# A graph layer's node products: from a scheduler's order to the order as written

## The chip, the cores and the metric

The kernel runs on one core of a Trainium2 chip. The metric is the device time of one launch in microseconds; the median of three timed runs of the kernel before is 6621.72 us (6620.99 to 6621.94). The profile was taken in an execution of its own, which with the profiler running spans 7287.9 us. Comparisons are made in timed runs; the profile serves to see where time lies.

Names of the engines: PE is TensorE (matmuls), PEld its loads of weights, DVE is VectorE, ACT is ScalarE, POOL is GpSimd, SP is SyncE, which only starts transfers here.

## The reference

10,000 nodes with 512 features, 160,000 edges sorted by destination, four edge types. Cut to what matters:

```python
# layer 0
h = relu(layernorm(x))
h_all = einsum('nd,rdf->nrf', h, rel_W) + rel_b        # four products for each node
agg = segment_sum(h_all[src, edge_type], dst) / max(deg, 1)
u = layernorm(h + h @ self_W + self_b + agg) * ln1_w + ln1_b
out = layernorm(u + gelu(u @ W1 + b1) @ W2 + b2) * ln2_w + ln2_b
x = x + out
# layer 1: two rounds of h <- relu(h @ W_self + mean of h[src] over a node's edges @ W_neigh + b)
x = x + layer1(relu(layernorm(x)))
```

All is in fp32. The nodes are handled in 79 blocks of 128 (the last has 16).

## The kernel before

It has four stages: (1) the node products, with the work on the edges put between them: for each block of nodes five products of 128x512 by 512x512, one with `self_W` and four with `rel_W`, whose results go to memory, and beside it the lists of rows that each block will gather; (2) gathering and summing for layer 0 and its feed-forward part; (3) and (4) the two rounds of layer 1, which gather again. Stages 2 to 4 are bound to the order in which they are written. Stage 1 isn't: a scheduler orders its instructions and puts each engine's queue together by its own model of their times.

The edge work is a Python generator: each `next(step)` emits the instructions up to the next `yield`. First `runs`, which finds where each node's edges begin, then `lists`. The parts of stage 1 that matter:

```python
    def runs(ep, ep2, pse, found):
        # ... loads of dst, dst shifted by one, src, etype
        yield
        # ... d_f, m, ends, bad: each wants the loads; then keys
        for i in range(ROUNDS):                     # ROUNDS = 12: the largest eight keys of a row, 12 times
            nc.vector.max(out=top[:, w], in_=key)
            # ... match_replace takes them out of key
            if i % 2:
                yield
        # ...
        pn = pse.tile([P, 512], F32, name="pe")
        for i in range(ROUNDS):                     # counting
            w = slice(8 * i, 8 * i + 8)
            inb = ep2.tile([P, 8, NB], F32, name="inb")
            nc.vector.tensor_tensor(inb, ..., op=OP.is_equal)
            inl = ep2.tile([P, 8, P], F32, name="inl")
            nc.vector.tensor_tensor(inl, ..., op=OP.is_equal)
            nc.vector.tensor_tensor(inl, inl, ..., op=OP.mult)
            for j in range(8):
                nc.tensor.matmul(pn[:NB, :P], inb[:, j, :], inl[:, j, :], start=(i + j == 0),
                                 stop=(i == ROUNDS - 1 and j == 7))
            if i % 2:
                yield
        # ... scans over the counts, bounds of each block, two levels, the test `fits`

    def look_up(b0, nb, win):                       # two blocks of the list
        # ... marks and own rows, on VectorE
        for c in range(nb):
            nt = OT if b0 + c < full else OT_LAST
            of = between(found["from"], found["upto"], b0 + c, nt * P, "of")     # two masks
            pm = pse.tile([P, OT, WT], F32, name="pe")
            for t in range(nt):
                nc.tensor.matmul(pm[:, t, :], of[:, t * P:(t + 1) * P],
                                 halves[:, c, 2 * t0:2 * t0 + WT], start=True, stop=True)
            got, rows, none = picked(pm[:, :nt], slot[:, :nt], 0, 2)             # eleven small operations
            nc.vector.tensor_tensor(loc[:, b0 + c, :nt], got[:, :, 1], none, op=OP.add)
            nc.vector.tensor_copy(orow[:, b0 + c, :nt], rows)
        # ...
        for c in range(nb):
            # ... kept <- a part of the window; masks `beyond` for two levels (4 and 16 blocks)
            #     at the last block of a level: share(lv, b)

    def share(lv, last):
        # ...
        for j in range(n):
            nc.tensor.matmul(pm[:, 0, :], beyond[lv][:, j, :], kept[0][:, (b1 + j) % SPAN, :],
                             start=(j == 0), stop=(j == n - 1))
        got, rows, none = picked(pm[:, :1], slot[:, :1], 64, 4 + 2 * lv)
        # ... stores to srow and loc
```

And the loop that drives it:

```python
        def products(g):
            b0, nb, r = g
            xg = loaded.pop()
            sc = norm_scales(ap_, [xg[:r, c, :] for c in range(nb)], r, "a")
            hg = xp.tile([P, 4, D], F32, name="hg")
            for c in range(nb):
                h = hg[:r, c, :]
                nc.scalar.activation(h, xg[:r, c, :], AF.Relu, bias=sc[c][1], scale=sc[c][0])
                hT = ap_.tile([P, KC, P], F32, name="hT")
                transposed(psT, hT[:, :, :r], h, r)
                nc.vector.tensor_tensor(h, h, bself[:r], op=OP.add)
                nc.vector.tensor_tensor(xg[:r, c, :], xg[:r, c, :], ln2b[:r], op=OP.add)
                ha = ap_.tile([P, R, D], F32, name="ha")
                for j, w in enumerate([wself] + wrel):
                    pm = psM.tile([P, D], F32, name="pm")
                    for k in range(KC):
                        nc.tensor.matmul(pm[:r], hT[:, k, :r], w[:, k, :], start=(k == 0),
                                         stop=(k == KC - 1))
                    if j:
                        nc.vector.tensor_tensor(ha[:r, j - 1, :], pm[:r],
                                                brel[:r, (j - 1) * D:j * D], op=OP.add)
                    else:
                        nc.vector.tensor_tensor(h, pm[:r], h, op=OP.add)
                n0 = (b0 + c) * P
                nc.scalar.dma_start(hall_d[n0:n0 + r, :], ha[:r].rearrange("p r d -> p (r d)"))
                gate[:] = [ha[:, 0, :1]] if r == P else []
                if b0 + c >= 2:
                    next(step, None)
            nc.sync.dma_start(rows_of(xs_d, g), hg[:r, :nb])
            nc.sync.dma_start(rows_of(xr_d, g), xg[:r, :nb])

        for g, later in zip(groups, groups[1:] + [None]):
            products(g)
            if later:
                load(later)
        gate.clear()
        for _ in step:
            pass
```

`norm_scales` is two statistics instructions per block on VectorE, a square root on ScalarE and two small instructions on VectorE for a group of four blocks; `transposed` is four transposes on TensorE and one copy on ScalarE. The accumulators `pm` have four buffers, `hT` and `ha` two each, the edge work's `pe` two.

After the stage every engine loads `fits`, the test whether the lists have room, and branches to stages 2 to 4:

```python
    go = nc.values_load(fits[0:1, 0:1], min_val=0, max_val=1, ...)
    with tc.If(go > 0) as cmp:
        with ExitStack() as ctxa:
            with tc.manual_schedule():
                aligned(ctxa)
```

Of the kernel before, what the change touches and what calls it, by code (L numbers as in the profile page):

```python
# [8 lines left out]
F32 = mybir.dt.float32  # L9
# [12 lines left out]
def kernel(  # L22
# [52 lines left out]


    T = 11 * E // (16 * N)
    OT = 5
    OT_LAST = 3
# [3 lines left out]

    ROUNDS = 12
    PAD = P

    W = 36
    TAGS = 4 + 3 * NL
    FAR = 2 * SPAN * P
    WT = 2 * W + TAGS  # L90
    assert N % P and R * N <= 1 << 16 and 2 * T + WT <= 2 * P and OT * WT <= 512
    assert (4 + 3 * NL) * NB <= 1024 and 3 * NL * NB <= 512
    assert 4 * OT * P <= R * N and OT_LAST < OT and full % 2 == 0

    def own(b):

        return T if b < full else 0

# [24 lines left out]


    row = const.tile([P, full, T], I32, name="row")
    orow = const.tile([P, NB, OT], I32, name="orow")
    srow = [const.tile([P, -(-full // n)], I32, name=f"srow{i}") for i, n in enumerate(SPANS)]
    loc = const.tile([P, NB, OT + NL], F32, name="loc")
# [41 lines left out]
    def runs(ep, ep2, pse, found):  # L170
# [32 lines left out]
        yield  # L203
# [30 lines left out]
        for i in range(ROUNDS):  # L234
            w = slice(8 * i, 8 * i + 8)
            nc.vector.max(out=top[:, w], in_=key)
            if i + 1 < ROUNDS:
                rest = ep2.tile([P, EC], F32, name="m")
                nc.vector.match_replace(out=rest, in_to_replace=top[:, w], in_values=key,
                                        imm_value=0.0)  # L240
                key = rest
            if i % 2:
                yield
# [29 lines left out]
        for i in range(ROUNDS):  # L273
# [14 lines left out]
            if i % 2:  # L288
                yield
# [18 lines left out]
        nc.vector.tensor_tensor(deg, first[:, 1:], first[:, :P], op=OP.subtract)  # L308

# [25 lines left out]
        bounds = ep.tile([NB, 3 * NL, P], F32, name="bounds")  # L335
        nc.vector.tensor_copy(first_over, over)
        done = 0
        for lv, n in enumerate(SPANS):
# [22 lines left out]
            for i, v in enumerate((ov, upto)):  # L361
                w = bounds[:, 3 * lv + i, :]
                nc.vector.tensor_scalar(w, bounds[:, 3 * lv - 3 + i, :] if lv else v,
                                        float(-P if lv else -OT * P), 0.0, op0=OP.add, op1=OP.max)
                nc.vector.tensor_scalar(w, w, skip, None, op0=OP.add)
            nc.vector.tensor_scalar(bounds[:, 3 * lv + 2, :], ov, shift, 64.0, op0=OP.add,
                                    op1=OP.add)
            nc.vector.tensor_scalar(bounds[:, 3 * lv + 2, :], bounds[:, 3 * lv + 2, :], 0.0, None,
                                    op0=OP.max)
            yield  # L370
        for names, vs in ((("first", "deg", "from", "upto"), (first[:, :P], deg, ov, upto)),
                          ([f"{k}{lv}" for lv in range(NL) for k in ("sfrom", "supto", "sbase")],
                           [bounds[:, i, :] for i in range(3 * NL)])):
# [6 lines left out]
        nc.vector.memset(bad[:, 3:5], 0.0)  # L380
# [3 lines left out]
        nc.vector.tensor_scalar(bad[:NB, 3:4], upto_b, float(-P), over, op0=OP.is_lt, op1=OP.add)  # L384
        nc.vector.tensor_reduce(room, deg, op=OP.max, axis=mybir.AxisListType.X)
        nc.vector.tensor_tensor(room, room, lanes_b, op=OP.subtract)
        nc.vector.tensor_scalar(bad[:NB, 4:5], room, float(W), None, op0=OP.is_gt)
        pf = pse.tile([P, 512], F32, name="pe")
        nc.tensor.matmul(pf[:1, :5], ones[:, :1], bad, start=True, stop=True)
        count = ep.tile([1, 1], F32, name="count")  # L390
        nc.vector.tensor_reduce(count, pf[:1, :5], op=OP.add, axis=mybir.AxisListType.X)
        nc.vector.tensor_scalar(fits, count, 0.0, None, op0=OP.is_equal)
# [4 lines left out]
    def lists(ep, ep2, pse, found):  # L397

        tags = ep.tile([P, NB, TAGS], F32, name="tags")
        tag_i = ep.tile([P, NB, TAGS - 2], I32, name="tag_i")  # L400
        nc.vector.memset(tags[:, :, 0:1], 1.0)
        nc.gpsimd.iota(tags[:, :, 1], pattern=[[0, NB]], base=0, channel_multiplier=1,
                       allow_small_or_imprecise_dtypes=True)
        for i, n in enumerate(SPANS):
            of = tag_i[:, :, 2 + 2 * NL + i]
            nc.gpsimd.iota(of, pattern=[[1, NB]], base=0, channel_multiplier=0)
            nc.vector.tensor_scalar(of, of, n - 1, None, op0=OP.bitwise_and)
        for i, name in enumerate(["from"] + [f"sbase{lv}" for lv in range(NL)]):
            hi, lo = tag_i[:, :, 2 * i], tag_i[:, :, 2 * i + 1]
            nc.vector.tensor_copy(lo, found[name])  # L410
            nc.vector.tensor_scalar(hi, lo, 4, None, op0=OP.logical_shift_right)
            nc.vector.tensor_scalar(lo, lo, 15, None, op0=OP.bitwise_and)
        nc.vector.tensor_copy(tags[:, :, 2:], tag_i)
        nc.vector.memset(orow[:, full:, :], 0)
        nc.vector.tensor_scalar(rdeg, found["deg"], 1.0, None, op0=OP.max)
        nc.vector.reciprocal(rdeg, rdeg)
        iota_s = ep.tile([P, OT * P], F32, name="iota_s")
        nc.gpsimd.iota(iota_s, pattern=[[1, OT * P]], base=0, channel_multiplier=0,
                       allow_small_or_imprecise_dtypes=True)
        of_span = ep.tile([P, SPAN], F32, name="of_span")  # L420
        nc.gpsimd.iota(of_span, pattern=[[P, SPAN]], base=0, channel_multiplier=0,
                       allow_small_or_imprecise_dtypes=True)
        slot = ep.tile([P, OT], F32, name="slot")
        nc.gpsimd.iota(slot, pattern=[[P, OT]], base=0, channel_multiplier=1,
# [73 lines left out]
        def look_up(b0, nb, win):  # L498
# [24 lines left out]
            if not t0:  # L523
                return
# [819 lines left out]
```

## Time and profile before

| | |
|---|---|
| timed, median | 6621.72 us |
| profiled span | 7287.9 us |
| first stage, to its last VectorE instruction | about 1578 us |
| busy over the whole span | PE 77%, DVE 50%, ACT 14%, POOL 52% |
| eviction of a product (`ha<-pm,brel`, 128x512) | 688 ns, x312 |
| bias addition (`hg<-hg,bself`) and residual addition (`xg<-xg,ln2b`) on DVE | 684 and 683 ns, x78 each |
| lookup mask (`of<-iota_s,f_upto,after`, 128x640) | 878 ns, x78 |

A group in the profile reads: line, engine, operation, output<-inputs, shape, count | busy us in all, mean ns of one | us that the engine stood idle before it <- what it waited for. A wait reads: engine, tile and line that waited <- who released it: total us, times, longest. A timeline row reads: start us, length us, engine, line, operation, count. The product matmuls are in fp32 and each appears as two records, so a product of four matmuls is eight records.

### The profile page before, as it was taken

To read this page: it belongs to the slowest core of one execution; us is meant where nothing else is said; L and a number is where in the kernel's file an instruction comes from. 1 tells how busy PE (TensorE), PEld (TensorE's weight loads), DVE (VectorE), ACT (ScalarE), POOL (GpSimd) and SP (SyncE) were. 2 spreads that over 40 slices of the span, in tenths; PEclk is the share of its full clock that TensorE was granted. 3 is DMA by queue.
4 is the path that set the end of the run, shared out by engine and by line. 5 is a ranking of instruction groups with operands and counts; after the bars stand their busy time and mean duration, and the time that the engine had idled before them with its cause. 6 is when DMAs were issued, how large, how long until landed. Compare 5 with 4: busy or idle time off the path is not lost.

```text
span 7287.9 us, 49954 instructions
## 1 busy us (share of the span) xinstructions
PE 5630.5 (77%) x14251; PEld 2543.5 (35%) x14251; DVE 3658.1 (50%) x7302; ACT 1016.8 (14%) x1667; POOL 3806.5 (52%) x3927
## 2 busy tenths in 40 slices
PE   8999999976899888897676666666666666666666
PEld 3444444433334333343333233333232233332232
DVE  5457777334666666665344344333333444444444
ACT  1000000002233223232211011001010000000000
POOL 0000010026666666666266666666656666666665
PEclk9999999987999999998888888888887888887888
DMA  4222222246677777776366666666666777777775
GB/s 156 101 99 99 104 94 93 93 142 191 214 222 225 227 218 225 225 228 207 125 199 207 207 207 208 207 207 204 207 205 206 218 220 218 218 217 216 221 220 171
DMA packets 456993, 1361.47 MB, mean 187 GB/s; under 512 B 71746, under 2 KB 71746, under 8 KB 446578
## 3 DMA queue, kind: packets, MB, share of 16 engines
q0 software_dynamic: 308768, 1008.91, 46.8%
q1 hardware_dynamic: 136146, 266.29, 10.3%
q10 hardware_dynamic: 11792, 82.97, 2.8%
q8 instruction: 114, 1.87, 0.1%
q14 instruction: 173, 1.42, 0.1%
HBM read 1150.89 MB, written 207.01 MB: 186 GB/s over the span
## 4 chain that ended last, share of the span: by engine, by line
PE 34%; issue 21%; another core or an unknown queue 19%; ACT 3%; DVE 3%; POOL 2%; DMA 2%; ACTq 0%; POOLq 0%; DVEq 0%; SPq 0%
PE pa L687 9%; PE ph L783 6%; PE pm L620 5%; PE po L794 5%; PE po L991 3%; PE po L1025 3%; DVE pa L699 2%; POOL rows L660 2%; PE pT L167 1%; ACT hTb L168 1%; DMA rows<-h_d,row 1%; ACT mTb L168 1%; ACT mb L1021 0%; PE pT L771 0%
## 5 line engine op out<-in xcount | busy, mean ns | idle before, releaser
L699 DVE TENSOR_TENSOR pa<-pa,rows 128x512 f32<-128x512 f32 x2574 | 1798.6, 699 | 906.1 <-issue 571.5
L660 POOL DMA_INDIRECT rows<-h_d,row x1716 | 1669.4, 973 | 906.0 <-issue 423.0
L1025 PE MATMUL po<-wss,hTb 128*128 128x512 f32 (+1 forms) x1264 | 710.5, 715 | 652.1 <-ACT hTb L168 536.3
L687 PE MATMUL pa<-rows,hot 128*128 128x512 f32 (+1 forms) x2358 | 1096.2, 611 | 55.5 <-issue 31.9
L660 POOL DMA_INDIRECT rows<-hall_d,row x858 | 855.9, 998 | 492.6 <-issue 196.3
L620 PE MATMUL pm<-wrel,hT 128*128 128x512 f32 (+1 forms) x2528 | 1101.0, 593 | 14.4 <-DVE ha L623 14.4
L991 PE MATMUL po<-wns,mTb 128*128 128x512 f32 (+1 forms) x1264 | 662.0, 673 | 439.0 <-ACT mTb L168 306.3
L660 POOL DMA_INDIRECT rows<-h_d,orow x786 | 754.6, 960 | 400.8 <-issue 218.9
L620 PEld LDWEIGHTS pm<-wrel,hT 128*128 128x128 f32 (+1 forms) x2528 | 478.0, 189 | 622.1 <-issue 595.9
L687 PEld LDWEIGHTS pa<-rows,hot 128*128 128x128 f32 (+1 forms) x2358 | 458.9, 195 | 665.2 <-issue 631.6
L783 PE MATMUL ph<-x1T,w1s 128*128 128x512 f32 (+2 forms) x1344 | 587.0, 590 | 117.9 <-ACT hid L785 88.4
L1025 PEld LDWEIGHTS po<-wss,hTb 128*128 128x128 f32 (+1 forms) x1264 | 277.8, 231 | 1024.0 <-ACT hTb L168 589.5
L660 POOL DMA_INDIRECT rows<-hall_d,orow x393 | 373.3, 950 | 450.3 <-SPq L1340 326.5
L794 PE MATMUL po<-w2s,hid 128*128 128x512 f32 (+1 forms) x1264 | 560.9, 595 | 30.5 <-issue 23.2
L991 PEld LDWEIGHTS po<-wns,mTb 128*128 128x128 f32 (+1 forms) x1264 | 266.8, 216 | 816.2 <-issue 483.0
L687 PE MATMUL pa<-tail,hot 128*128 128x512 f32 x936 | 469.0, 617 | 78.0 <-issue 72.7
L997 DVE TENSOR_TENSOR po<-po,bss 128x512 f32<-128x512 f32 (+1 forms) x79 | 55.0, 696 | 805.5 <-remote 705.9
L493 POOL DMA_INDIRECT win<-rec_d,at x79 | 74.9, 948 | 719.7 <-issue 631.4
L623 DVE TENSOR_TENSOR ha<-pm,brel 128x512 f32<-128x512 f32 (+1 forms) x316 | 217.1, 687 | 424.1 <-PE pm L620 424.0
L783 PEld LDWEIGHTS ph<-x1T,w1s 128*128 128x128 f32 x1344 | 259.8, 201 | 414.1 <-issue 311.4
L1001 DVE TENSOR_TENSOR ob<-po,bss 128x512 f32<-128x512 f32 (+1 forms) x79 | 54.5, 689 | 663.4 <-remote 293.6
L794 PEld LDWEIGHTS po<-w2s,hid 128*128 128x128 f32 (+1 forms) x1264 | 236.2, 190 | 313.4 <-issue 301.8
(238 smaller groups left out, 4165.3 us busy)
## 6 DMA issues: line engine op xcount, KB each, us to landing
hall_d<-ha ACTq DMA_DIRECT2D x78, 1024.0 KB
hb<-h_d SPq DMA_DIRECT2D x38, 1024.0 KB
rows<-h_d,row POOLq DMA_INDIRECT x1716
xs<-xs_d SPq DMA_DIRECT2D x39, 512.0 KB
xr<-xr_d SPq DMA_DIRECT2D x39, 512.0 KB
xn_d<-xr SPq DMA_DIRECT2D x39, 512.0 KB
h_d<-h SPq DMA_DIRECT2D x39, 512.0 KB
xg<-in_x_dram SPq DMA_DIRECT2D x19, 1024.0 KB
```

What stands on the lines that cost most here:

```text
L167: nc.tensor.transpose(p[:, k, :r], rows[:, k * P:(k + 1) * P], ident[:r, :r])
L168: nc.scalar.copy(dest, p[:, :, :r])
L493: nc.gpsimd.indirect_dma_start(out=win[:, c, :], out_offset=None, in_=rec_d, in_offset=bass.IndirectOffsetOnAxis(ap=at[:, c:c + 1], axis=0))
L620: nc.tensor.matmul(pm[:r], hT[:, k, :r], w[:, k, :], start=(k == 0), stop=(k == KC - 1))
L623: nc.vector.tensor_tensor(ha[:r, j - 1, :], pm[:r], brel[:r, (j - 1) * D:j * D], op=OP.add)
L660: nc.gpsimd.indirect_dma_start(out=t[:n], out_offset=None, in_=table, in_offset=bass.IndirectOffsetOnAxis(ap=idx, axis=0))
L687: nc.tensor.matmul(pa[:r], hot[:, t, :r], others[t], start=(t == order[0]), stop=(t == order[-1]))
L699: nc.vector.tensor_tensor(pa[:r], pa[:r], t[:r], op=OP.add)
L783: nc.tensor.matmul(ph[:, :n], w1s[:, k, f * P:(f + 1) * P], self.xT[:, k, :n], start=(k == 0), stop=(k == KC - 1))
L794: nc.tensor.matmul(po[:r], self.hid[:, f, c * r:(c + 1) * r], w2s[:, f, :], start=(f == 0), stop=(f == FC - 1))
L991: nc.tensor.matmul(po[:r], mT[:, k, :r], wns[:, k, :], start=False, stop=(k == KC - 1))
L1025: nc.tensor.matmul(po[:r], hT[:, k, :r], wss[:, k, :], start=(k == 0), stop=False)
```

## The change

It makes the first stage follow the order in which it is written (`manual_schedule`), and rewrites the loop for it: a block's products come one after another; behind product 0 the next block's norm is prepared, behind product 1 the norm is applied, behind product 3 the next block is transposed; behind products 0, 2 and 4 a piece of edge work is put. The additions of `bself` and of `ln2b` go to GpSimd. The stores of `ha` go from ScalarE's queue to SyncE's. It is meant to keep TensorE going from product to product.

```diff
     with ExitStack() as s:
+        s.enter_context(tc.manual_schedule())
 ... (load, then three new helpers)
+        def stats(g, c):
+
+            if c == 0:
+                scales[g] = norm_scales(ap_, [xgs[g][:g[2], k, :] for k in range(g[1])], g[2], "a")
+
+        def normed(g, c):
+            r = g[2]
+            if c == 0:
+                hgs[g] = xp.tile([P, 4, D], F32, name="hg")
+            nc.scalar.activation(hgs[g][:r, c, :], xgs[g][:r, c, :], AF.Relu, bias=scales[g][c][1],
+                                 scale=scales[g][c][0])
+            nc.gpsimd.tensor_tensor(xgs[g][:r, c, :], xgs[g][:r, c, :], ln2b[:r], op=OP.add)
+
+        def turned(g, c):
+            r = g[2]
+            hTs[g, c] = ap_.tile([P, KC, P], F32, name="hT")
+            transposed(psT, hTs[g, c][:, :, :r], hgs[g][:r, c, :], r)
 ... (products(g) and its loop go)

+        for do in (stats, normed, turned):
+            do(*seq[0])
+        for i, (g, c) in enumerate(seq):
+            n0 = (b0 + c) * P
+            if c == 0 and i + nb < len(seq):
+                load(seq[i + nb][0])
+
+            ahead = {0: stats, 1: normed, 3: turned} if i + 1 < len(seq) else {}
+            h, hT = hgs[g][:r, c, :], hTs.pop((g, c))
+            ha = ap_.tile([P, R, D], F32, name="ha")
+            for j, w in enumerate([wself] + wrel):
+                pm = psM.tile([P, D], F32, name="pm")
+                for k in range(KC):
+                    nc.tensor.matmul(pm[:r], hT[:, k, :r], w[:, k, :], start=(k == 0),
+                                     stop=(k == KC - 1))
+                if j in ahead:
+                    ahead[j](*seq[i + 1])
+                if j:
+                    nc.vector.tensor_tensor(ha[:r, j - 1, :], pm[:r],
+                                            brel[:r, (j - 1) * D:j * D], op=OP.add)
+                else:
+                    nc.vector.tensor_tensor(h, pm[:r], h, op=OP.add)
+                    nc.gpsimd.tensor_tensor(h, h, bself[:r], op=OP.add)
+                if i >= 3 and j % 2 == 0:
                     next(step, None)
+            nc.sync.dma_start(hall_d[n0:n0 + r, :], ha[:r].rearrange("p r d -> p (r d)"))
+            if i == 2:
+                gate[:] = [ha[:, 0, :1]]
+            if c == nb - 1:
+                nc.sync.dma_start(rows_of(xs_d, g), hgs[g][:r, :nb])
+                nc.sync.dma_start(rows_of(xr_d, g), xgs[g][:r, :nb])
```

The edge work is cut into smaller pieces. In `runs`, ten empty pieces stand behind the loads, and both loops over the rounds yield each time:

```diff
-        yield
+        for _ in range(10):
+            yield
 ...
-            if i % 2:
-                yield
+            yield
```

`look_up` becomes two steps for each block, `start` (all its masks) and `finish` (the matmuls and what follows), each a piece of its own:

```diff
+        def finish(self, b, of, window):
+
+            ls = self.ls
+            t0, nt = 2 * ls.own(b), ls.others(b)
+            window = window[:, t0:t0 + ls.WT]
+            pm = self.bank()
+            for t in range(nt):
+                nc.tensor.matmul(pm[:, t, :], of[:, t * P:(t + 1) * P], window, start=True, stop=True)
+            got, rows, none = self.picked(pm[:, :nt], self.slot[:, :nt], 0, 2)
+            nc.vector.tensor_tensor(ls.loc[:, b, :nt], got[:, :, 1], none, op=OP.add)
+            nc.vector.tensor_copy(ls.orow[:, b, :nt], rows)
+            if b == full:
+                return
+            j = b % SPAN
+            if j == 0:
+                self.kept = self.ep.tile([P, SPAN, ls.WT], BF16, name="kept")
+            nc.vector.tensor_copy(self.kept[:, j, :], window)
+            for lv, span in enumerate(SPANS):
+                if b % span == span - 1 or b == full - 1:
+                    self.share(lv, b)
 ...
         def look_up(b0, nb, win):
-            halves = win.rearrange("p b j -> p (b j)").bitcast(BF16).rearrange(
-                "p (b j) -> p b j", b=2)[:, :nb]
 ...
+            halves = halves_of(win, nb)
+            look.mark(b0, nb, halves)
+            if b0 < full:
+                look.mine(b0, nb, halves, found["deg"])
+            of = []
             for c in range(nb):
 ...
+                of.append(look.start(b0 + c))
+                yield
             for c in range(nb):
 ...
+                look.finish(b0 + c, of[c], halves[:, c, :])
+                yield
 ...
         ahead = []
         for b in range(0, NB, 2):
             ahead.append(read(b))
             if len(ahead) > 3:
-                look_up(*ahead.pop(0))
+                yield from look_up(*ahead.pop(0))
             yield
         while ahead:
-            look_up(*ahead.pop(0))
-            yield
```

The test `fits`, computed behind the bounds before, is computed in a last piece behind the lists:

```diff
+    def room(ep, pse):
+
+        pf = pse.tile([P, 512], F32, name="pe")
+        nc.tensor.matmul(pf[:1, :5], ones[:, :1], bad, start=True, stop=True)
+        count = ep.tile([1, 1], F32, name="count")
+        nc.vector.tensor_reduce(count, pf[:1, :5], op=OP.add, axis=mybir.AxisListType.X)
+        nc.vector.tensor_scalar(fits, count, 0.0, None, op0=OP.is_equal)
+        yield
```

The rest of the diff gathers the sizes of a list into a class and passes it along; stages 2 to 4 keep their operations and their order.

## The prediction

> **What bounds the kernel now.** I read the page's slices first, then the windows, the groups by shape, TensorE's waits, and at last the timeline of TensorE and of VectorE. All of the change lies in the first stage, the node products, which end at 1578 us of a profiled span of 7288 us (the timed median is 6621.7 us). The page's first two rows of slices:
>
> ```profile
> PE   8999999976899888897676666666666666666666
> ...
> PEclk9999999987999999998888888888887888887888
> ```
>
> One slice is 182 us, so the stage is the first eight to nine digits: TensorE is at nine tenths at nearly full clock. The windows split the stage (columns: us; busy us and instructions of PE, PEld, DVE, ACT, POOL; clock; DMA share; GB/s):
>
> ```profile
> 300.00:420.00 120.00, 119.35 (x416) 63.24 (x414) 55.79 (x80) 8.72 (x14) 0.00 (x0) 1.00 0.23 88
> 600.00:800.00 200.00, 185.04 (x564) 85.55 (x563) 148.16 (x626) 11.82 (x20) 17.80 (x19) 0.96 0.24 91
> 1400.00:1500.00 100.00, 99.12 (x248) 44.93 (x247) 23.82 (x37) 5.04 (x8) 0.00 (x0) 1.00 0.19 79
> ```
>
> With little VectorE work TensorE idles under 1%; between 600 and 1200 us, where the lists of edges are looked up, it idles 7.5%. TensorE sets this stage, VectorE is at 75% at most. The stage's TensorE waits, from 20 us to 1578 us:
>
> ```profile
> PE pe L518 <- DVE both L466: 53.5, 18, 3.3
> PE pm L620 <- DVE ha L623: 14.4, 1, 14.4
> PE pm L620 <- ACT hT L168: 9.4, 15, 5.2
> PE pe L547 <- DVE both L466: 3.2, 4, 2.5
> ```
>
> That is 80.5 us: all that a perfect order could give back directly. What one stop does is seen in TensorE's timeline:
>
> ```profile
> 817.22 0.52 PE L518 MATMUL pe<-win,of 128*128 128x82 bf16 x5 [2.95 <-DVE both L466]
> 817.54 5.10 PE L620 MATMUL pm<-wself,hT 128*128 128x512 f32 x8
> 822.48 13.90 PE L620 MATMUL pm<-wrel,hT 128*128 128x512 f32 x32
> 859.25 0.36 PE L518 MATMUL pe<-win,of 128*128 128x82 bf16 x5 [2.95 <-DVE both L466]
> 859.45 3.67 PE L620 MATMUL pm<-wself,hT 128*128 128x512 f32 x8
> ```
>
> A product is 8 records, 3.43 us. After a stop of 2.95 us the next takes 5.1 to 5.4 us in 14 of 18 cases and 3.67 us in the others: a stop costs itself and mostly 1.6 us of slower clock.
>
> **What the Trainium skill says.** "TensorE: Matmul & The Clock Gate", Part 1: the array falls to half clock after an idle window of about 3.4 us and needs a busy one to return; a product of twice the time for part of a window is what the lines above show. "PSUM — Partial Sum Buffer", Engine vs sequencer instructions: VectorE, ScalarE and GpSimd queues are strict FIFO and matmuls start in program order; so an edge matmul that waits for VectorE holds all products behind it. The later stages of this kernel, already written out by hand, show VectorE in exactly the written order. "GPSIMD Engine Reference", 3.1 Elementwise: a two-input fp32 addition takes GpSimd 1.96 times VectorE's time; with 0.69 us here an estimate is 1.35 us, and no such addition of GpSimd is in this trace. "SBUF — State Buffer", two separate sides: such an addition excludes a VectorE instruction with two SBUF inputs while it runs; not shown in this trace either.
>
> **What the change removes.** (1) The four waits: 80.5 us. Transposes of the next block come after product 3 and are copied during product 4; the lookup is split so that its masks are made at least one product before the matmul that needs them; ten empty steps cover the load of the edges, for which VectorE stood 22.7 us while TensorE lost 14.4. (2) Slow restarts: 14 x 1.65 = 23 us, and 2.8 us after the long stop (9.83 us for 16 records instead of 7.03): 26 us. (3) Two additions of 0.68 us per block leave VectorE: 79 x 1.37 = 108 us of busy time, worth nothing directly, as VectorE isn't the bound. Sum: 106 us.
>
> **What it adds.** The order as written puts each piece of edge work on VectorE behind the eviction of the product just made, and the piece's matmuls on TensorE before the next product. Where a piece makes a matmul's operand in the same piece, TensorE now stands through a round trip. The rows that price it:
>
> ```profile
> L283 DVE TENSOR_TENSOR inl<-inl,end_f 128x1024 f32<-128x1024 f32 x12 | 14.6, 1217 | 0.1
> L280 DVE TENSOR_TENSOR inl<-lane,to_f 128x1024 f32<-128x1024 f32 x12 | 14.6, 1217 | 0.0
> L276 DVE TENSOR_TENSOR inb<-lane,blk_f 128x632 f32<-128x632 f32 x12 | 9.8, 813 | 4.6 <-PE pe L286 4.6
> ```
>
> (a) The twelve rounds of counting. Eviction starts 0.20 us after the next product could, occupies 0.60; the three instructions start 0.74, 1.25 and 1.22 us apart, as 315.03, 318.02 and 319.27 us of the timeline show; 0.04 to the matmul: 4.05 us of lost products, x 12 = 49 us. Before, the scheduler made the operands one round ahead and TensorE lost nothing (119.35 of 120 us).
>
> (b) The steps from counts to bounds: three VectorE-TensorE round trips, and two for the levels: about 1.6 + 0.7 + 0.9 + 4.3 + 1.5 = 9 us from scans of 0.42 us and small instructions of 0.15 to 0.3 us.
>
> (c) The shared tails. Once in four blocks the piece that finishes a block goes on to a sum over `kept`, whose last part is copied by the last instruction of that piece. Chain behind the eviction (0.80 us): got 0.20, nth twice 0.16, pick 0.34, both 0.53, two reductions 0.33 overlapping to 0.62, five small ones of 0.16 of which three in a chain, two stores and the copy 0.18, with 0.04 between dependent ones: 3.0 us. Less the 0.19 us of the block's own matmuls: 3.7 us lost. 18 of 20 fall inside the stage: 67 us. The second level comes straight behind and finds its operands ready.
>
> (d) Collisions: some of these pieces stand at product 0, where the norm of a group (about 4 us) or GpSimd's addition (1.35 us) is in the way. Three or four shared tails and a third of the rounds: 8 us, a guess.
>
> (e) Slow restarts after 12 + 4 + 18 = 34 stops, at the rate seen now (26 us for 19 stops, 1.4 each): 47 us.
>
> (f) The end. I counted the pieces. The first part has 10 + 3 + 12 + 1 + 12 + 3 = 41, the lists 1 + 40 + 39 x 4 + 2 = 199, the last test 1: 241. Slots: blocks 3 to 78, three each, 228. Thirteen pieces are left when the last product is done: finishing six blocks, beginning five, three shared tails, the test. Six finishes of 3.4 us (the chain and its matmuls), five beginnings of 1.3 to 2.6 us (0.55 + 0.88 us for the large masks, twice 0.29 + 0.34 for the small, 0.4 for marks and rows) make 10.7, three shared tails 2.8, test 1: 41 us. The gathers and the branch wait for that test, which today is known at 457 us, and the first gather comes 3.8 us after the last eviction:
>
> ```profile
> 1577.63 0.68 DVE L623 TENSOR_TENSOR ha<-pm,brel 16x512 f32<-16x512 f32 x1 [2.75 <-PE pm L620]
> 1587.72 0.69 DVE L750 TENSOR_TENSOR lnb<-lnb,h 128x512 f32<-128x512 f32 x1 [9.41 <-DMA ln1wc<-in_L_gnn_ln_w_dram]
> ```
>
> Sum added: 49 + 9 + 67 + 8 + 47 + 41 = 221 us. Net: 221 - 106 = +115 us. The later stages are the same code and only start later: 6622 + 115 = about 6736 us, 1.7% slower.
>
> **The rivals.** *It gains.* If TensorE doesn't really wait in (a) and (c), because queues run ahead or the pieces' operands are ready, only the 106 us remain against a tail: 6622 - 106 + 41 = 6557 us, 1% faster. For it speaks that lookup matmuls were deliberately separated from their masks; against it that counting rounds and shared tails were not. *VectorE falls behind.* If pieces take longer than the gaps between products, four accumulators fill and TensorE stops more: lists need 11 us of VectorE per five pieces, that is 6.6 us per block, with 3.5 us of evictions and 1 us of norm 11 of 18 us; so no lasting backlog, only (d). If it happened, another 40 us: 6780. *The end is hidden.* If the leftovers overlap the last products, or GpSimd's gathers are slow to start anyway, (f) vanishes: 6695. Against: the branch waits for the test, and no part of the gathering stage can begin before it. *Nothing changes*, as the time is set by the gathers: against, because a later start moves everything behind it.
>
> **Range and chances.** (a) and (c) are the firm part, from counted pieces and measured durations; (d), (e) and the overlap inside (f) carry perhaps 20 us each, and the step that TensorE waits at all could fail, but rarely. 8 in 10: 6670 to 6790. The line for 2% is 6754 us, 18 us above my number, so slower by over 2% has 0.36; faster by over 2% would take 132 us, more than all that can be removed: 0.02; within 2%: 0.62.
>
> **What would show it.** In the profile after: the stage ends near 1690 us instead of 1578; TensorE's waits no longer name the lookup's matmul behind the reduction, nor the transposed block, but the counting matmul behind its operands 12 times near 4 us, and the shared sum behind `kept` 18 times near 3.7; the last eviction of a product is followed by some 41 us with TensorE nearly empty and VectorE busy. I am wrong if those stops are absent or short, if the lists are done before the last product, or if the stages behind differ in length by more than some 20 us.

## The result and the profile after

| | before | after |
|---|---|---|
| timed, median | 6621.35 us (6615.35 to 6621.94) | 6777.56 us (6775.24 to 6778.60) |
| last eviction of a product begins | 1577.63 us | 1687.02 us |
| first gather begins | 1582.08 us | 1733.10 us |
| TensorE's stops while it makes products | 80.5 us | 152.2 us |

The change makes the kernel slower: the ratio is 1.0238 (95%: 1.022 to 1.0255), +156 us where +115 was predicted. The first gather, with which the first stage ends, begins 151.0 us later. The stages behind it take 5043.8 us; a second profile of the kernel before has 5039.8 us there. One caution for all that follows: the stages behind the first gather took 5.04 ms on some chips and 5.7 ms on others whichever kernel ran (in the first profile of before 5.7 ms), so variants are compared with before on their own chip in timed runs, and by the start of the first gather in the profiles. The 7287.9 us that stand ahead of the prediction as the profiled span are of this kind and don't come of the profiler: before takes 7285 and 7332 us in timed runs on two of the chips used below, and 6617 to 6628 us on the two others. On the first two the same microseconds make a ratio that is a tenth nearer to 1.

The slices of the page of after (169 us each, the first stage is the first ten and a part of the eleventh):

```profile
PE   8789999998499999999977777777777777777777
...
PEclk9889999999699999999988898888888888898888
```

Two places have changed: the second digit, where the rounds are counted, has fallen to 7 at a lower clock, and the eleventh (1694 to 1863 us) is at 4, with a clock of 6: it holds 39 us without products, in which TensorE waits for the lists, and then the beginning of the gathering. Windows of the two (us; busy us and instructions of PE, PEld, DVE, ACT, POOL; clock; DMA share; GB/s):

```profile
220.00:450.00 230.00, 165.23 (x479) 93.44 (x479) 92.21 (x181) 9.29 (x15) 23.14 (x22) 0.82 0.16 60
...
1687.00:1733.00 46.00, 5.27 (x55) 3.38 (x55) 38.42 (x180) 0.00 (x0) 0.00 (x0) 0.55 0.05 6
```

In the second, VectorE is busy for 38.4 of 46 us and TensorE for 5.3: the edge work that was left over is a chain on VectorE with nothing beside it. TensorE's waits from 20 us to the last eviction (line and tile that waited, who released it, total us, times, longest):

```profile
PE pe L554 <- DVE kept L542: 82.2, 21, 5.6
PE pe L299 <- DVE inl L296: 55.0, 12, 6.0
PE pe L375 <- DVE by L373: 4.0, 1, 4.0
PE pT L180 <- ACT hg L668: 3.2, 1, 3.2
```

The waits that stood in before's list are gone, and the two of the prediction's (a) and (c) stand first: `inl`, 12 times, and `kept`, at 18 shared tails. Three of these wait three times in a row, first 0.67 us for `both` (2.0 us in all, not in the lines above), then 1.34 and 4.05 us for `kept`. What such a stop looks like, in TensorE's timeline of the rounds:

```profile
229.29 3.60 PE L698 MATMUL pm<-wrel,hT 128*128 128x512 f32 x8
236.79 2.60 PE L299 MATMUL pe<-inl,inb 128*79 128x128 f32 x16 [3.90 <-DVE inl L296]
239.18 4.70 PE L698 MATMUL pm<-wself,hT 128*128 128x512 f32 x8
249.85 3.70 PE L299 MATMUL pe<-inl,inb 128*79 128x128 f32 x16 [5.97 <-DVE inl L296]
```

Eight of the twelve stops are 3.90 us, four are 5.97. The work behind a stop runs slower: the sixteen records of a round take 2.60 and 3.70 us, and the product behind the first 4.70 us instead of 3.60. Why four stops are longer is seen in VectorE's timeline, with a last operand of an undisturbed round (235 us) and two of the round behind the second stop, and in GpSimd's at the same time:

```profile
235.51 1.22 DVE L296 TENSOR_TENSOR inl<-inl,end_f 128x1024 f32<-128x1024 f32 x1
...
245.31 2.28 DVE L293 TENSOR_TENSOR inl<-lane,to_f 128x1024 f32<-128x1024 f32 x1
247.63 2.17 DVE L296 TENSOR_TENSOR inl<-inl,end_f 128x1024 f32<-128x1024 f32 x1
```

```profile
244.75 1.76 POOL L707 TENSOR_TENSOR hg<-hg,bself 128x512 f32<-128x512 f32 x1 [19.14 <-DVE hg L706]
246.47 2.24 POOL L670 TENSOR_TENSOR xg<-xg,ln2b 128x512 f32<-128x512 f32 x1
```

At product 0 GpSimd's two additions run at the same time as the piece, and each VectorE instruction beside one takes about 1 us longer. At a shared tail behind product 0 it is the same, with small instructions. TensorE's stop, and VectorE's `nth` in an undisturbed piece (576 us) and in the one that stops TensorE (580 us):

```profile
584.92 0.23 PE L554 MATMUL pe<-kept,beyond 128*128 128x82 bf16 x1 [5.61 <-DVE kept L542]
```

```profile
576.14 0.17 DVE L476 SCALAR_TENSOR_TENSOR nth<-got,slot 128x5 f32<-128x5 f32 x1
...
579.90 1.21 DVE L476 SCALAR_TENSOR_TENSOR nth<-got,slot 128x5 f32<-128x5 f32 x1
581.14 1.19 DVE L478 SCALAR_TENSOR_TENSOR nth<-nth,got 128x5 f32<-128x5 f32 x1
```

Five elements per partition take 1.21 us while an addition of GpSimd lasts (579.82 to 581.08 and 581.04 to 582.30 us in its timeline). The two together make a tail 2.07 us longer: 5.62 instead of 3.55 us.

The +151.0 us add up so. TensorE's stops: 152.2 - 80.5 = +71.7 us. From the last eviction to the first gather: 46.08 - 4.45 = +41.6 us. The rest is slower products: the products of the stage (79 x 40 records at 0.4293 us) and the other matmuls make 1441.5 us at full clock; with the first 14.5 us, in which there is nothing to multiply yet, and the stops taken off, 79 us remain after and 41 before: +38 us. Whether that rest is the clock, and what each stop carries, is for the experiments.

### The profile page after: what moved, and what is told of

The parts are those of the page before. It is cut to its first block, busy times and chain, and to the rows that moved or that the text cites. A ratio compares the mean times of both kernels' runs of the same rounds, so it can differ in the third digit from the quotient of the medians.

```text
span 6776.9 us, 50035 instructions
## 1 busy us (share of the span) xinstructions
PE 5697.4 (84%) x14251; PEld 2513.2 (37%) x14251; DVE 3769.1 (56%) x7104; ACT 1013.3 (15%) x1667; POOL 4037.2 (60%) x4085
## 4 chain that ended last, share of the span: by engine, by line
PE 45%; DMA 36%; DVE 8%; issue 5%; POOL 5%; ACT 1%; another core or an unknown queue 0%; POOLq 0%; DVEq 0%; ACTq 0%; SPq 0%
PE pm L698 20%; DMA rows<-h_d,row 19%; DMA rows<-h_d,orow 11%; PE pa L764 7%; PE ph L856 6%; PE po L867 5%; POOL rows L736 5%; DMA rows<-hall_d,row 4%; PE po L1098 3%; DVE pa L772 2%; PE po L1064 2%; PE pT L180 1%; DMA rows<-hall_d,orow 1%; PE pe L299 1%; DMA tail<-h_d,srow 1%
## 5 line engine op out<-in xcount | busy, mean ns | idle before, releaser
L764 PE MATMUL pa<-rows,hot 128*128 128x512 f32 (+1 forms) x2358 | 1374.5, 721 | 672.7 <-DMA rows<-h_d,orow 609.5
L698 PE MATMUL pm<-wrel,hT 128*128 128x512 f32 (+1 forms) x2528 | 1151.4, 607 | 0.0
L764 PEld LDWEIGHTS pa<-rows,hot 128*128 128x128 f32 (+1 forms) x2358 | 492.7, 225 | 1545.1 <-DMA rows<-h_d,orow 1082.6
L736 POOL DMA_INDIRECT rows<-h_d,orow x786 | 786.1, 1000 | 357.8 <-issue 123.0
L707 POOL TENSOR_TENSOR hg<-hg,bself 128x512 f32<-128x512 f32 (+1 forms) x79 | 106.2, 1344 | 1081.3 <-DVE hg L706 781.1
L1064 PE MATMUL po<-wns,mTb 128*128 128x512 f32 (+1 forms) x1264 | 572.3, 596 | 1.5 <-ACT mTb L181 1.5
L1098 PE MATMUL po<-wss,hTb 128*128 128x512 f32 (+1 forms) x1264 | 571.2, 595 | 0.0
L1094 ACT ACTIVATE mb<-pa,rdeg 128x512 f32<-128x512 f32 (+1 forms) x158 | 108.5, 687 | 1831.9 <-DVE pa L772 1824.0
L1098 PEld LDWEIGHTS po<-wss,hTb 128*128 128x128 f32 (+1 forms) x1264 | 228.1, 191 | 230.6 <-issue 230.5
L698 PE MATMUL pm<-wself,hT 128*128 128x512 f32 (+1 forms) x632 | 307.7, 632 | 0.7 <-ACT hT L181 0.7
```

Source lines behind the costliest of these rows:

```text
L707: nc.gpsimd.tensor_tensor(h, h, bself[:r], op=OP.add)
L736: nc.gpsimd.indirect_dma_start(out=t[:n], out_offset=None, in_=table, in_offset=bass.IndirectOffsetOnAxis(ap=idx, axis=0))
L764: nc.tensor.matmul(pa[:r], hot[:, t, :r], others[t], start=(t == order[0]), stop=(t == order[-1]))
L1064: nc.tensor.matmul(po[:r], mT[:, k, :r], wns[:, k, :], start=False, stop=(k == KC - 1))
L1094: nc.scalar.activation(m[:r], pa[:r], AF.Copy, scale=rdeg[:r, b:b + 1])
L1098: nc.tensor.matmul(po[:r], hT[:, k, :r], wss[:, k, :], start=(k == 0), stop=False)
```

## The experiments

The theory: the slowdown is the order as written where a piece makes an operand and uses it in the same piece (rounds and shared tails), each stop costing itself and a slow restart; then the leftover pieces at the end; then GpSimd's additions beside VectorE. The rivals: VectorE as such is too far behind (then undoing one place only moves the stop elsewhere); the slow products have another cause than the stops; the additions on GpSimd are what costs. The stores of `ha` on SyncE's queue and the later test `fits` were not undone by themselves; the run without `manual_schedule` has both and is faster than before.

### The rounds one ahead

Piece i makes the operands of round i and multiplies those of round i - 1; one of the ten empty pieces is dropped, so the number of pieces stays.

```diff
-        for i in range(ROUNDS):
+        for i in range(ROUNDS + 1):          # operands of round i (if i < ROUNDS) are made, then
-            nc.tensor.matmul(pn[:NB, :P], inb[:, j, :], inl[:, j, :], ...)
+            nc.tensor.matmul(pn[:NB, :P], pb[:, j, :], pl[:, j, :], ...)   # those of round i - 1
```

> The counting rounds make their operands one piece ahead of the matmuls that use them; nothing else changes (one empty piece less keeps the number of pieces). If TensorE stands because the operands are made in the same piece, the 12 stops (55 us) go, and with them the slow clock behind them (31 us in that stretch): about 86 us less, 6692 us. If the stops only move elsewhere, because VectorE is behind anyway, the time stays within 20 us of 6778.

The first gather moved from 1733.10 to 1646.43 us, -86.7 us: 58.2 us of stops (55.0 in the rounds, and the 3.2 of the transpose that waited for `hg`) and 28.5 of slow products. Timed: 1.0074 (1.0054 to 1.0095) of before. TensorE's timeline of this kernel:

```profile
230.64 1.91 PE L304 MATMUL pe<-inl,inb 128*79 128x128 f32 x16
232.39 3.60 PE L703 MATMUL pm<-wself,hT 128*128 128x512 f32 x8
```

The stop is gone, the round takes 1.91 us and the product 3.60. VectorE makes the same operands with the same instructions as in after, so it was the distance between making and using that cost, and not VectorE's load.

### The shared sums in a piece of their own

A shared sum is no longer begun at the end of `finish`, but in the next empty piece of the lists.

```diff
                 if b % span == span - 1 or b == full - 1:
-                    self.share(lv, b)
+                    self.due.append((lv, b))
 ...
                 look.finish(b0 + c, of[c], halves[:, c, :])
                 yield
+            while look.due:
+                look.share(*look.due.pop(0))
```

> The shared tails are summed in the piece after the one that copies into kept, which is empty as the change has it. If the wait for kept is the cause, 84 us of stops go and some 38 us of slow clock: about 120 us less, 6657 us. The rival, a VectorE that is behind in this stretch, keeps most of it: over 6740 us.

First gather at 1608.89 us, -124.2: 84.2 us of stops and 40.0 of slow products. Timed: 1.0028 (1.001 to 1.0046). The same place of the lists in TensorE's timeline:

```profile
580.97 0.32 PE L554 MATMUL pe<-kept,beyond 128*128 128x82 bf16 x4
581.13 3.67 PE L700 MATMUL pm<-wrel,hT 128*128 128x512 f32 x8
```

Between 700 and 1000 us TensorE is now busy for 299.93 of 300 us at a clock of 1.00; in after it was 278.12 at 0.96. This edit alone takes back 80% of the loss.

### Stops filled with a product

To part the stop from the slow restart: ahead of the edge matmuls of a round or of a first-level share, the next product is computed once more than needed, on operands that are there, so that TensorE works where it would stand. Thirty such products, 3.43 us each, are added work.

```diff
+            for fill in busy:                # the coming product, computed one extra time
+                fill()
             for j in range(8):
                 nc.tensor.matmul(pn[:NB, :P], inb[:, j, :], inl[:, j, :], ...)
```

> The stops stay, but TensorE is given a product to compute in each of them (the next one, computed twice, 8 records of 0.43 us), in the rounds and in the shared tails. No useful work is added and nothing is left out. If a stop costs itself and then a slow clock, the slow part goes: 40 to 70 us less, 6708 to 6738 us, with more matmuls in all. If the slow products behind the stops had another cause than TensorE's idling, the time stays or grows by up to 10 us.

First gather at 1678.11 us, -55.0. In the stage the rounds' stops fell from 55.0 to 13.9 us and the tails' from 84.2 to 22.2: 103 us less. Timed: 1.0117 (1.0089 to 1.0145) of before. The added products take 30 x 3.43 = 103 us, so the two cancel, and the 55 us are slow clock alone. TensorE's timeline of a round, with the added product just ahead of the first row:

```profile
241.28 1.97 PE L301 MATMUL pe<-inl,inb 128*79 128x128 f32 x16 [0.47 <-DVE inl L296]
243.09 3.60 PE L663 MATMUL pm<-wself,hT 128*128 128x512 f32 x8
```

The round is nearly and the product behind it wholly at full speed (1.97 and 3.60 us; in after 2.60 and 4.70). So the slow products came from the idle time, and not from the edge work beside them.

### No empty pieces in the lists

Every second step of the lists ends with an empty piece; 37 of the 241 go, so that the lists fit the 228 places.

```diff
             if len(ahead) > 3:
                 yield from look_up(*ahead.pop(0))
-            yield
+            else:
+                yield
```

> The empty piece after each pair of blocks in the lists is dropped, so that 204 pieces stand against 228 places and the lists end before the last product. If the 13 pieces left over stand alone on the path to the branch, about 40 us go: 6737 us. If the branch had something else to wait for, such as the stores of the products, little goes: 6765 us or more.

A miss: first gather at 1724.06 us, -9.0; timed 1.0207 (1.019 to 1.0224) of before. The end did shrink, from 46.1 to 5.1 us, but the last eviction came 31.9 us later. The stops at `kept` went from 82 to 106.5 us (20 of them, as all tails now lie in the stage), and six are 9.46 us long. The chain ahead of one, from VectorE's timeline and then TensorE's:

```profile
565.28 0.68 DVE L168 BATCH_NORM_STATS2 sta<-xg 128x6 f32<-128x512 f32 x1
...
569.22 0.68 DVE L707 TENSOR_TENSOR hg<-pm,hg 128x512 f32<-128x512 f32 x1
569.82 0.20 DVE L471 COPY got<-pe 128x50 f32<-128x50 f32 x1
570.06 1.21 DVE L476 SCALAR_TENSOR_TENSOR nth<-got,slot 128x5 f32<-128x5 f32 x1
```

```profile
575.08 0.23 PE L554 MATMUL pe<-kept,beyond 128*128 128x82 bf16 x1 [9.46 <-DVE kept L542]
```

The tail now follows directly behind another full piece, then the norm of a whole group (565.28 to 569.22 us, 3.9 us), then GpSimd's 2.07 us: 3.55 + 3.9 + 2.07 = 9.5 us. The end was paid for with denser pieces and their collisions. So the empty pieces were not only slack at the end, but also where VectorE caught up.

### No empty pieces, and places behind products 1, 2 and 4

Is it the coincidence at product 0, or the density? The edit is the one above with `j % 2 == 0` replaced by `j in (1, 2, 4)`.

> The empty pieces dropped, and the pieces behind products 1, 2 and 4. Dropping them alone brought the first gather only from 1733 to 1724 us, because every third shared tail then fell behind the norm of a group and GpSimd's additions at product 0 and stood 9.46 us. If it was that coincidence, no stop is above about 4 us here and the end without leftovers counts in full: first gather at about 1693 - 41 + 11 (two shared tails more inside) = 1663 us, and the time some 30 us under that of the pieces behind 1, 2 and 4 alone, 6712 us. If denser pieces leave VectorE behind at any place, stops of 6 us and more stay, and the gather starts after 1680 us.

First gather at 1674.65 us, between the two answers; timed 1.0115 (1.0068 to 1.0161) of before. Six of twenty tails still wait 6.08 us. In them the piece no longer stands behind product 0, but the norm that does still ends late (547.4 us, in VectorE's timeline ahead of a stop) and two evictions are queued behind it, to 548.6 us. Product 0's eviction is one of them, so GpSimd's addition comes late as well and meets this piece's two `nth`, which take 0.61 and 1.19 us instead of 0.17. Of the 2.5 us above 3.55, 1.5 are this and some 1.0 the late start. The coincidence was the larger part of the miss (9.46 became 6.08 us). The rest goes with density, as the piece has another close ahead of it and no empty one to catch up in; this is read from the timeline and was not tried by itself.

### The additions on VectorE again

```diff
-            nc.gpsimd.tensor_tensor(...)     # both additions
+            nc.vector.tensor_tensor(...)
```

> The two additions per block go back to VectorE, at the same places in the order. If GpSimd's additions hold up VectorE's small work behind product 0 (stops of 5.97 instead of 3.90 us, four in the rounds and six in the shared tails), those ten shrink by about 1.4 us each and the slow clock a little: 10 to 25 us less, 6755 us. If VectorE's load is what counts, 1.2 us more of it per block makes the time longer: up to 6800 us.

First gather at 1714.26 us, -18.8; timed 1.0191 (1.0174 to 1.0208) of before. The four long rounds went from 5.97 to 4.63 us and the six long tails from 5.62 to 4.23. Doing the additions on VectorE costs 1.37 us per block there and is still better: at product 0 one of them stands in front of the piece, but no small instruction is held (no `nth` takes more than 0.17 us in this run).

### Places behind products 1, 2 and 4

```diff
-                if i >= 3 and j % 2 == 0:
+                if i >= 3 and j in (1, 2, 4):
```

> The pieces stand behind products 1, 2 and 4 instead of 0, 2 and 4, so that GpSimd's additions, which follow product 0, run beside no piece. If it is the additions that lengthen the stops to 5.97 and 5.62 us, no stop is above about 4 us and 20 us go, with less of a slow clock 20 to 35 us: 6745 to 6758 us. If the longer stops come from the place behind product 0 itself (the norm of the group), they stay, or move to product 1, and the time is within 10 us of 6778.

First gather at 1693.47 us, -39.6 (somewhat more than the bound expected); timed 1.0169 (1.0152 to 1.0186). All twelve rounds wait 3.90 us, 12 x 3.90 = 46.8 us, and the six tails that waited 5.62 us now wait 3.55. Three tails still stop three times in a row, for 0.68, 1.34 and 3.43 us, which is 5.45 us together:

```profile
634.66 0.23 PE L554 MATMUL pe<-kept,beyond 128*128 128x82 bf16 x1 [3.43 <-DVE kept L542]
```

In each of them the piece one product ahead stood behind the norm of a group (in the first to 625.2 us of VectorE's timeline), so its own copy into `kept` began only at 630.8 us. Of the 39.6 us, 8.2 are the rounds' stops, some 15 the tails', 2.8 the transpose that waited for `hg`, 2.0 the bounds; the rest is clock. So what product 0 adds to the stops is about as dear as the whole end, (f).

### Only the additions, in the kernel before

The two lines of the additions on GpSimd, in the kernel before, with its scheduler.

> The kernel before with one part of the change: the two additions on GpSimd, under the scheduler. If VectorE has time to spare and the scheduler hides what is blocked, the time is within 15 us of 6621. If the additions block VectorE when the lookup needs it, it is 20 to 60 us longer.

First gather at 1623.42 us, +38.3 against the second profile of before; timed 1.0053 (1.0036 to 1.007), +37 us. The wait that stood first in before, there at 53.5 us, and a row of VectorE's timeline ahead of one of its stops:

```profile
PE pe L518 <- DVE both L466: 83.4, 18, 4.6
...
692.67 1.22 DVE L460 SCALAR_TENSOR_TENSOR nth<-nth,got 128x5 f32<-128x5 f32 x1
```

The stops became longer, from 2.95 (one 3.31) to 4.63 us, and ahead of every one of the 18 one `nth` takes 1.22 or 1.23 us instead of 0.16. VectorE wasn't the bound on average; but these instructions lie in the chain that TensorE waits for, and this is where a time is set. The stops make 27 of the 38 us.

### The change without the order as written

`manual_schedule` is dropped; loop, pieces and GpSimd additions stay, and the scheduler orders them.

```diff
-        s.enter_context(tc.manual_schedule())
```

> The changed kernel without its first line: the scheduler orders the first stage again, all else is as changed. If the order as written is what brings the stops, they go and the time is near that of before, 6600 to 6640 us. If the pieces themselves, or the additions on GpSimd, are the cause, it stays above 6720 us.

First gather at 1512.96 us, -220 us against after and -70 against before; timed 0.9893 (0.9877 to 0.991). This is better than expected. TensorE's stops from 20 us to the last eviction are few, 21.7 us:

```profile
PE pm L697 <- DVE ha L702: 13.6, 1, 13.6
PE pm L697 <- ACT hT L181: 3.6, 1, 3.6
PE pe L323 <- DVE first L318: 3.3, 1, 3.3
```

The rounds and `kept` are gone from the list. So the rest of the change, taken together, is a gain under the scheduler, even with 29 us of leftovers at the end (last eviction 1483.77 us); what lost was the written order, together with pieces that use what they have just made.

### Four mends together, as written and scheduled

Rounds one ahead, shared sums in their own piece only when one is due, no empty pieces (223 for 228 places), places behind products 1, 2 and 4; in the order as written.

> Order as written, with the rounds one piece ahead, the shared tails in a piece of their own, the empty pieces dropped (223 pieces for 228 places) and the pieces behind products 1, 2 and 4. If the accounts above are right, nearly nothing but matmuls is left on TensorE in the first stage: 1442 us of matmuls at full clock, some 15 us at the start and 10 to 20 of round trips in the bounds, so the first gather starts at about 1480 us instead of 1582: 6505 to 6535 us, 1.3 to 1.8% under the kernel before. If the gathers behind it, not the products, set the end, it stays at 6620 us or above.

First gather at 1479.69 us; timed 6515.06 us (6510.09 to 6517.85) against 6616.73: 0.9844 (0.9831 to 0.9858), 1.6% faster than before, and so also than after. From 450 us to the last eviction (columns as above):

```profile
450.00:1474.00 1024.00, 1023.88 (x3013) 466.14 (x3011) 711.87 (x2433) 77.56 (x126) 209.69 (x179) 1.00 0.28 105
```

TensorE idles 0.12 us of 1024, at full clock, though VectorE is at 70% and GpSimd still makes the additions. The savings of the separate runs add up: rounds -86.7, shares -124.2 and, of the end, 46.1 - 5.1 = -41.0 make -251.9 us; measured -253.4. The gain of other places (-39.6 alone) isn't added: it lay for the most part in the length of stops that are no longer there.

The same kernel with the scheduler:

> The version with all four mends, but ordered by the scheduler instead of as written. The first gather was at 1480 us as written, and the matmuls alone need 1442 us behind a start of 14 us. If the pieces decide, now that none makes and uses an operand at once, either order ends within 15 us of 1480 us: a time of 6500 to 6535 us. If the scheduler gathers edge work again as it did in the kernel before, stops of 3 us in the lookup come back: 1500 us or more, 6540 us or more.

First gather at 1489.82 us, 10 us later, with one stop of 13.5 us (the load of the edges) that the scheduler has again; timed 0.9858 (0.9813 to 0.9902) of before on its chip. The intervals of the two overlap. With operands made a piece ahead, no cost of the order as written against the scheduler's is left that these runs can show.

### The kernel before once more

To see whether the length of the stages behind the first gather, 5706 us in the first profile of before and 5044 in that of after, comes of the change.

> The kernel before, profiled once more. Its three later stages took 5706 us in the first profile but 6621 - 1582 = 5039 us by the timed runs, and 5044 us in the changed kernel's profile. If the first profile was drawn out by the profiler, this one has a span near 6620 us and the first gather again at about 1582 us; if the change really shortened the later stages, the span is near 7290 us again.

First gather at 1585.08 us and 5039.8 us behind it, in a span of 6624.9 us. The later stages are as long as in after; the difference was not the change's.

## Why the prediction was right in direction and short in size

The result, 6777.56 us, lies in the range of 6670 to 6790, above the 6736 predicted. The mechanism held: TensorE stands where a piece uses what it has just made, and the lists end after the products. Two terms were too small.

| step of the prediction | predicted us | measured us |
|---|---|---|
| (1) waits removed | -80.5 | -80.5, none is left |
| (2) slow restarts removed | -26 | about -37 |
| (a) twelve rounds | 49 | 46.8 (12 x 3.90), without what product 0 adds |
| (b) bounds | 9 | 9.8 |
| (c) shared tails | 67 | 64 (18 x 3.55) |
| (d) collisions | 8 | about 31 |
| (e) slow restarts added | 47 | about 75 |
| (f) end | 41 | 41.6 |
| sum at the first gather | 115 | 151 |

- **(a), (b), (c) and (f)**, counted pieces by durations of the profile before, are each within 3 us; they carried the prediction. In (c) the terms as listed make 3.6 us for one tail and not the 3.7 written; 3.55 were measured.
- **(d) is the first term that was mis-sized**, and the text called it a guess. Measured: 8.2 us in the rounds (55.0 - 46.8), 20 in the tails (84.2 - 64), 3.2 at the transposes. The prediction saw both colliding parties, and a third of the rounds was right, but nine tails were hit and not three or four (six at product 0, three just behind the norm), and it treated GpSimd's additions as 1.35 us in all: there are two in a row (the estimate for one was right, 1344 ns in the mean of 79), and each holds a small two-input instruction of VectorE nearly to its end. The Trainium skill, "SBUF — State Buffer", two separate sides, says just this, that the second to start is blocked for the whole instruction; the trace agrees, with 1.21 us for an `nth` that begins 0.08 us into an addition of 1.26. The prediction named it and then priced part (3) at nothing, because VectorE isn't the bound; the additions alone cost +37 us in before, with its scheduler.
- **(e) is the second.** Of the 79 us of slow products after, the rounds carry 28.5 (2.4 each) and the tails 40.0 (2.2 each), by the two runs that took their stops away. Two stops in the bounds carry some 6: the product behind the first of them takes 6.56 us. That makes about 75 and leaves about 4 that no stop explains. If the same 4 stood in before, its stops carried 41 - 4 = 37 us, and not the 26 of (2). The net is +38 us, where 47 - 26 = 21 was predicted. Part of this is a reading: the prediction took the product behind the first lookup stop, the only one of 3.31 us, for a fast one, and left out those behind a stop of 5.15 us at `hT` (5.88 us) and behind one at the second level. Before's timeline:

```profile
569.02 0.52 PE L518 MATMUL pe<-win,of 128*128 128x82 bf16 x5 [3.31 <-DVE both L466]
569.34 6.31 PE L620 MATMUL pm<-wself,hT 128*128 128x512 f32 x8
```

The rate of before is thus about 1.8 us per stop and not 1.4, and that of the longer stops after is higher again. The trace agrees with "TensorE: Matmul & The Clock Gate", Part 1, in that idle time halves the speed for a while: behind such stops the records of a product start 0.85 us apart instead of 0.43. The idle window of about 3.4 us that the page gives is not a lower limit for a single stop here: of the 17 lookup stops of 2.95 us in before, 14 were followed by slow products.
- **The rivals.** "It gains" fell with the order as written, but is what happens as soon as TensorE needn't wait: the run without `manual_schedule`, 1.1% faster, and the four mends, 1.6%. "VectorE falls behind" is wrong of after as a whole (two single edits of the order take the stops away with VectorE's work unchanged), and right in one place, at pieces that follow a group's norm closely: three tails of after stop for 6.1 us for this reason, and where the pieces are dense, the run without empty pieces lost at the stops what it won at the end. "The end is hidden" fell: 46.1 us stand in the trace. "Nothing changes" fell: the later stages are as long as before, and start later.
- **The chances.** Slower by over 2% came in, and had 0.36. The line stood 18 us above the number, and the two uncertain terms leaned one way, as one was taken from the mildest stops and the other was a low count; the chance should have been near one half.
- **Where the 8 in 10 came from.** The prediction said 20 us each for (d) and (e); they were off by 23 and, net of (2), by 17, both in the same direction, so that the sum came 12 us short of the range's end.

What stays open: the length of a slow restart by the length of its stop was not measured by itself, only in groups; three of the 17 equal stops in before have no slow product behind them, and no run shows why; and why the later stages take 5.04 or 5.7 ms was not tried.

## What to carry to other kernels

Before fixing an order by hand, go through the pieces for an operand that is made and used in the same piece: here each such place cost the whole round trip, 3.55 to 6 us, and on TensorE a slow restart of 2.2 to 2.4 us more. Moving the use one piece later took back 211 us of the 253 that lie between the change and the version with four mends, without taking away any work. Then count pieces against places, so that none are left for the end. As long as some pieces still use at once what they make, empty ones between them are room for VectorE to catch up behind long instructions such as a group's norm; without such pieces, in the version with four mends, TensorE idles for 0.12 of 1024 us where the lists are made. And before work goes to GpSimd because VectorE is busy, see which VectorE chain it will run beside: the waits of the engine that sets the time lengthen by the held instructions, even though VectorE was busy for only 75% of the stretch.

## What the runs showed of the hardware that was not expected

- While GpSimd adds two 128x512 fp32 tiles (1.26 us each for most, 1344 ns in the mean of 79), a VectorE instruction on 5 elements per partition takes 1.21 us instead of 0.17, and ones on 1024 elements 2.28 and 2.17 instead of 1.22. GpSimd's own additions lengthen as well, to 1.76 and 2.24 us.
- Twelve TensorE stops of 3.9 to 6 us, with one or two products between them, lowered the mean granted clock between 220 and 450 us to 0.82, where before has 1.00, and the loss beside the stops themselves was 28.5 us. Filling the stops with products that nobody needs gave 55 us back, at no change of the sum of stops and work.
